# Attention scores: 64x64 TensorE tiles for each head's first 64 channels, 32-row tiles for the last 16

## The chip, the core and the metric

The kernel runs on one core of one Trainium2 chip. Five engines work side by side and meet at semaphores: TensorE (PE, matrix products, with its weight loads listed apart as PEld), VectorE (DVE), ScalarE (ACT), GpSimd (POOL) and SyncE (SP, which issues most DMAs). The metric is the device time of one execution in microseconds. TensorE multiplies a stationary operand, the weights, with a moving operand that streams through; the result goes to PSUM, whose banks are named s_ps, q_ps and so on here. A product may use only a part of the array's rows and columns, a tile, and products on different tiles may run side by side.

## What is computed

For each of 16 batch elements: 100 queries of width 640 attend over 718 keys of width 384 with 8 heads of 80 channels, a second attention over 4 extra tokens is added, and an output projection, a bias and the input follow.

```python
query = hidden_states @ Wq
keyt = enc @ Wk
valt = enc @ Wv
hs = _mha(query, keyt, valt)          # 8 heads, softmax over 718 keys
...
ca_hs2 = _mha(ca_q2, ca_k2, ca_v2)    # the 4 tokens
out = hs + ca_hs2
out = out @ Wout + b_out
out = out + residual
```

The change concerns `scores = einsum('bhqd,bhkd->bhqk', qh, kh)` inside the first `_mha`: for each head, 80 channels of the query times 80 channels of each key.

## The kernel before

All data are float32, and a float32 product appears in the trace as two TensorE records. The order of all instructions on all engines is written out by hand in the source: what stands earlier is issued earlier on its engine.

**Layout of the 640 channels.** Queries and keys are held with channels on the 128 partitions, in five chunks of 128. The columns of Wq and the rows of the transposed Wk (`wkt`) are permuted so that a chunk holds what the score products need. In chunks 0 to 3 a band of 32 partitions holds 32 of a head's first 64 channels: `packed` (line 104) puts heads 2r and 2r+1 into band r, the even one into chunks 0 and 1, the odd one into chunks 2 and 3. Chunk 4 holds the last 16 channels of all eight heads, so that a band of 32 partitions has two heads.

**Start.** `load_heads` (line 299) issues eight DMAs of 64 rows of `wkt`, alternating between the queues of ScalarE and SP; one more DMA on SP (line 307) brings chunk 4. `turn_back` (line 586) transposes each chunk of `wkt` on TensorE into w_ps, `first_keys` multiplies the first element's context with them. The permuted copies of Wq into `wq_sb` (lines 1277 to 1289) are made on ScalarE, two copies of 256 columns and one of 128 for each of five row chunks. DMAs take eight semaphores in turn, and a DMA waits for the one that had its semaphore before.

**One batch element.** `queries` (line 540) makes the projected queries of two elements: `qp` for chunks 0 to 3 and `qz` for chunk 4. `qz` holds two versions of the queries side by side, each with the other head's channels set to zero, so one product with 200 columns serves both heads of a band. Keys lie in six chunks of 120 (`KC`). `scores` (line 646) runs three times for each element, g = 0, 1, 2, and each time covers two key chunks, a = 0, 1. For each a it goes through the five channel chunks and the four bands: in chunks 0 to 3 a product with 32 rows, 120 key columns as weights and 100 streamed query columns, in chunk 4 one with 200 streamed columns. Band r always writes PSUM bank r, in which heads 2r and 2r+1 lie side by side; a call has 40 products. Groups 0 and 2 use two pairs of banks from the same pool, which ScalarE copies to `st` in two copies (line 688); group 1 uses four other banks and four copies (line 682).

After the scores come z_ps and y_ps of the second attention, then the blocks of keys (`k_ps`, line 470) and values (`v_ps`, line 439) in a fixed interleaving, then r_ps (line 1546) and a_ps (line 1564), which multiply the exponentials `st` with the values: r_ps in tiles of 32 weight columns, four at a time, for the last 16 channels and the sums, a_ps in tiles of 64 weight columns, two at a time. VectorE takes the maximum over the score tiles (lines 1416 and 1407) and subtracts it (line 1395); ScalarE makes the exponentials (line 1403).

Of the kernel before, what the change touches and what calls it, by code (L numbers as in the profile page):

```python
# [14 lines left out]
B, S, H = 16, 100, 640  # L15
NH, D = 8, 80
CAD, T = 384, 4
SK = 722 - T
P = 128
HC = H // P  # L20
# [3 lines left out]
KN = KT // 2  # L24
# [3 lines left out]
KEYS = [KN if j == 0 or u == 2 else KN - 1 for u, j in KC]  # L28
# [31 lines left out]
for h in range(NH):  # L60
    lo = h * D
    while lo < (h + 1) * D:
        c = lo // P
        hi = min((h + 1) * D, (c + 1) * P)
        PIECES.append((h, c, lo - h * D, lo - c * P, hi - lo))
        lo = hi
# [18 lines left out]
RG = 4  # L85
# [15 lines left out]
            )  # L101


def packed(to, w, h):

    rows = w.rearrange("(h k) n -> h k n", h=NH)
    at, c = 32 * (h // 2), 2 * (h % 2)
    return {
        "out": to[at : at + 32, c : c + 2],
        "in_": rows[h, :64].rearrange("(v k) n -> k v n", v=2),  # L110
    }


V_PLAN = [
# [33 lines left out]
def kernel(  # L148
# [18 lines left out]
    nc = tc.nc  # L167
# [22 lines left out]
    def pair(name):  # L190
        tile = ps2.tile([P, 2, 512], F32, tag="ps2", name=name)
        return tile
# [21 lines left out]
    def scores_tile(name):  # L214
        return main.tile([P, 2, ROWS], F32, tag="st", name=name, bufs=NP)
# [55 lines left out]
    def a_form(enc, f):  # L271
        return enc[0][:, A_AT[f]]
# [4 lines left out]
    wq_sb = const.tile([P, HC, H], F32, name="wq_sb")  # L277
    kT = const.tile([P, HC, 3, KT], F32, name="kT")
# [11 lines left out]
    wkt_sb = kT.rearrange("p c u k -> p c (u k)")[:, :, :CAD]  # L290
# [6 lines left out]
        )  # L297

    def load_heads(u):
        for h in range(u, NH, 2):  # L300
            (nc.scalar, nc.sync)[h // 2 % 2].dma_start(**packed(wkt_sb, wkt, h))

    load_heads(0)
    load_first(nc.sync, 0, 0)
    load_first(nc.scalar, 1, 0)
    load_first(nc.sync, 2, 0)
    load_heads(1)
    nc.sync.dma_start(
        out=wkt_sb[:, 4], in_=wkt.rearrange("(h k) n -> h k n", h=NH)[:, 64:]
    )  # L310
    for c in range(1, CC):
        for u in range(3):
            load_first(nc.sync, u, c)
# [9 lines left out]
        out=wv_sb[:, : 2 * CC].rearrange("p (c g) n -> p c (g n)", g=2),  # L323
        in_=wv.rearrange("(c p) n -> p c n", p=P),
# [6 lines left out]
    wq_in = [t[:, :H] for t in halves]  # L331
# [9 lines left out]
    def slot(i, h, lo, n):  # L341

        u, j = KC[i]
        lo += h % 4 * SLOT
        return vs.rearrange("p j k h n -> p j k (h n)")[: KEYS[i], j, 2 * u + h // 4, lo : lo + n]
# [16 lines left out]
    for h, c, r, s, k in PIECES:  # L362
        nc.gpsimd.dma_start(
            out=m2[s : s + k, c, GROUPS[c][1].index(-1), h * T : (h + 1) * T],
            in_=wqcat[h * D + r : h * D + r + k, :],
# [4 lines left out]
    for c in range(HC):  # L370
        first = c * P - HEADS[c][0] * D
        nc.gpsimd.affine_select(
            out=hmask[:, c], in_=hmask[:, c], compare_op=ALU.is_ge, fill=0.0,
# [3 lines left out]
            out=hmask[:, c], in_=hmask[:, c], compare_op=ALU.is_ge, fill=0.0,  # L377
# [37 lines left out]
    class Values(Blocks):  # L415
# [17 lines left out]
        def product(self, at, f, first, last):  # L433
            for bank in "AB":
                if self.opened[bank] is at and bank in self.fresh:
                    first = True
                    self.fresh.discard(bank)
            for j in range(2):
                nc.tensor.matmul(  # L439
                    at[0][j][:KN, : H // 2],  # L440
                    a_form(self.enc, f)[:, j * KN : (j + 1) * KN],
                    wv_sb[:, W_AT[f]],
                    start=first,
                    stop=last,
                    skip_group_check=True,
                )
# [199 lines left out]
    def scores(b, g, tiles):  # L646

        qp, qz = tiles
        name = f"s_ps_{b}_{g}"
        if g == 1:  # L650
            s_ps = [f(f"{name}_{r}") for r, f in enumerate((psumk, psumk, psum1, psum1))]
        else:
            pairs = [pair(f"{name}_{i}") for i in range(2)]
            s_ps = [pairs[r // 2][:, r % 2] for r in range(RG)]
        n = KN
        opened = set()

        def product(a, c, rows, bank, lo, rhs, last):
            u, j = KC[2 * g + a]
            nc.tensor.matmul(  # L660
                s_ps[bank][:n, 256 * a + lo : 256 * a + lo + rhs.shape[-1]],
                kT[rows, c, u, j * KN : (j + 1) * KN],
                rhs,
                start=bank not in opened,
                stop=last,
                skip_group_check=True,
            )
            opened.add(bank)

        for a in range(2):  # L670
            for c in range(HC):
                for r in range(RG):
                    rows = slice(32 * r, 32 * r + 32)
                    if c < HC - 1:
                        rhs = qp[rows, c // 2, c % 2, (b % 2) * S : (b % 2 + 1) * S]
                        product(a, c, rows, r, c // 2 * S, rhs, False)
                    else:
                        product(a, c, rows, r, 0, qz[rows, 0, b % 2], True)
        st = scores_tile(f"st_{b}_{g}")[:n]
        if g == 1:  # L680
            for r in range(RG):
                nc.scalar.copy(  # L682
                    st[:, :, 2 * r * S : 2 * (r + 1) * S],
                    s_ps[r][:n].rearrange("p (a q) -> p a q", a=2)[:, :, : 2 * S],
                )
        else:
            for i in range(2):
                nc.scalar.copy(  # L688
                    st[:, :, 4 * i * S : 4 * (i + 1) * S].rearrange(
                        "p a (r q) -> p r a q", r=2  # L690
                    ),
                    pairs[i][:n].rearrange("p r (a q) -> p r a q", a=2)[:, :, :, : 2 * S],
                )
        return st
# [580 lines left out]
        del gaps[:n]  # L1275

    for c in range(HC):
        for u in range(2):
            nc.scalar.copy(
                wq_sb[:, c, 2 * u * P : 2 * (u + 1) * P].rearrange(  # L1280
                    "p (v r k) -> p r v k", v=2, r=RG
                ),
                wq_in[c].rearrange("p (r u k) -> p r u k", r=RG, u=2)[
                    :, :, u, :64
                ].rearrange("p r (v k) -> p r v k", v=2),
            )
        nc.scalar.copy(
            wq_sb[:, c, 4 * P :].rearrange("p (h k) -> p h k", h=NH),
            wq_in[c].rearrange("p (h k) -> p h k", h=NH)[:, :, 64:],
        )  # L1290

    k2_ps = psum("k2_ps")
    for n in range(HC):
        for c in range(CC):
            for lo in (0, 64):
# [4 lines left out]
                    start=(c == 0),  # L1300
                    stop=(c == CC - 1),
                )
    k2T, at = [], 0
# [14 lines left out]
    for c in range(HC):  # L1318
        m_ps = psum(f"m_ps_{c}")
        for n, heads in enumerate(HEADS):  # L1320
# [4 lines left out]
                start=(n == 0),  # L1325
# [31 lines left out]
    for c in range(HC):  # L1357
        for half in range(2):
            h = 2 * c + half
            for cc in range(CC):  # L1360
                if c < HC - 1:
                    lo = h * D + FIRST[half]
                    weights = wvca_sb[:, cc, lo : lo + 64]
                else:
# [5 lines left out]
                    start=(cc == 0),  # L1370
# [5 lines left out]
    last, late, second_next = None, False, Second(1, xT)  # L1376
    for b in range(B):
        p = b // 2
# [13 lines left out]
        st = []  # L1392
# [12 lines left out]
        def larger(i):  # L1405
# [4 lines left out]
            return most_now  # L1410

        st.append(scores(b, 0, tiles))
        waiting = late
        if late:
            now.exponentials1()
        nc.vector.tensor_tensor(most[:KN], st[0][:, 0], st[0][:, 1], ALU.max)  # L1416
        st.append(scores(b, 1, tiles))
        larger(1)
        if b == 0:
            now.exponentials1()  # L1420
        st.append(scores(b, 2, tiles))

        vv = Values(b, e_in, V_PLAN if b + 1 < B else END_PLAN)
# [118 lines left out]
        for i in order:  # L1542
            for e in range(2):
                for h in range(e, NH, 2):
                    at = 16 * (h - e)
                    nc.tensor.matmul(  # L1546
                        rests[at : at + 32, e],
                        slot(i, h, -16 if e else 64, 32),
                        st[i // 2][: KEYS[i], i % 2, h * S : (h + 1) * S],
                        start=(i == order[0] and e == 0),  # L1550
                        stop=(i == order[-1]),
                        skip_group_check=True,
                    )
# [7 lines left out]
        for i in range(len(KC)):  # L1561
            for h in range(NH):
                e = h % 2
                nc.tensor.matmul(  # L1564
                    wides[64 * e : 64 * e + 64, h // 2],
                    slot(i, h, FIRST[e], 64),
                    st[i // 2][: KEYS[i], i % 2, h * S : (h + 1) * S],
                    start=(i == 0 and h // 2 == 0),
                    stop=(i == len(KC) - 1),
                    skip_group_check=True,  # L1570
                )
# [9 lines left out]
        last = mine  # L1581
# [52 lines left out]
```

## Time and profile before

| | us |
|---|---|
| three timed runs: median (lowest to highest) | 921.77 (920.55 to 922.27) |
| profiled execution: its own time | 921.04 |
| profiled execution: span of the trace | 919.3 |

A page of the profile gives busy time by engine, then the chain of work that ended last, then groups of instructions. In a group's row stand the line, the engine, the operation, out<-in by name, the rows*columns of the weights, the shape of the moving operand, the count, then busy time in us and the mean of one in ns. Busy time is the time in which at least one such instruction ran; with several tiles at once it is far below count times mean. Rows of the chain and of the timeline begin with the start and the length in us. A matmul's recorded length contains its way through the array; how fast matmuls follow one another is read from starts and counts.

### The profile page before, as it was taken

Reading aid. Unit: us, or ns where it says so; the run is one execution under the profiler, and the core shown is the slowest. Engines: PE = TensorE matmul, PEld = TensorE weight load, DVE = VectorE, ACT = ScalarE, POOL = GpSimd, SP = SyncE. Lnnn points to the kernel's source line nnn. Section 1 sums busy time; section 2 is a strip of 40 time slices with the busy share of each in tenths; the row PEclk is TensorE's granted clock in tenths of the full one; section 3 lists DMA queues with packets and bytes.
Section 4 is the critical chain, followed back from the end, with each engine's and each line's share of the span. In section 5 each row is a group of like instructions: output and inputs, shape, how many; then the busy total and the mean of one; then the engine's idle time right before and its main releaser. Section 6 shows DMA issues by size and latency. Waiting matters only on the chain.

```text
span 919.3 us, 26076 instructions
## 1 busy us (share of the span) xinstructions
PE 912.0 (99%) x11155; PEld 776.6 (84%) x11155; DVE 665.5 (72%) x1121; ACT 376.6 (41%) x654; POOL 620.6 (68%) x653
## 2 busy tenths in 40 slices
PE   8999999999999999999999999999999999999998
PEld 8988889797887979888798788988888888888865
DVE  3898795979639696675957759579782887828773
ACT  2354533544324443433434334344541445425351
POOL 9665786677847788476774756755796566955735
PEclk9999999999999999999999999999999999999999
DMA  9604351141402313140221403205140151401312
GB/s 288 218 11 133 66 123 34 29 120 39 103 12 70 106 25 90 43 132 12 72 72 43 132 12 81 71 6 134 43 110 11 34 140 36 111 11 45 86 53 64
DMA packets 68060, 69.50 MB, mean 76 GB/s; under 512 B 25192, under 2 KB 61352, under 8 KB 67944
## 3 DMA queue, kind: packets, MB, share of 16 engines
q1 hardware_dynamic: 67016, 66.97, 27.2%
q8 instruction: 88, 1.44, 0.7%
q10 hardware_dynamic: 464, 0.52, 0.2%
q0 software_dynamic: 464, 0.34, 0.2%
q14 instruction: 28, 0.23, 0.1%
HBM read 62.14 MB, written 8.94 MB: 77 GB/s over the span
## 4 chain that ended last, share of the span: by engine, by line
PE 97%; DMA 1%; POOL 1%; ACT 0%; DVE 0%; issue 0%; ACTq 0%; SPq 0%; DVEq 0%; POOLq 0%
PE s_ps L660 12%; PE v_psA L439 11%; PE v_psB L439 9%; PE k_psA L470 8%; PE a_ps L1564 7%; PE q_ps L544 7%; PE k_psB L470 7%; PE kT_ps L568 6%; PE r_ps L1546 4%; PE v_psC L439 4%; PE k_psC L470 3%; PE y_ps L799 2%; PE v_psD L439 2%; PE o_psy L1128 2%; PE v_psE L439 2%; PE k_psE L470 1%
## 5 line engine op out<-in xcount | busy, mean ns | idle before, releaser
L834 POOL TENSOR_TENSOR e<-ca,g 100x800 f32<-100x800 f32 x60 | 91.8, 1540 | 101.0 <-DVE most L1407 74.3
L439 PE MATMUL v_psA<-wv_sb,enc 128*120 128x320 f32 x384 | 119.6, 434 | 0.0
L507 POOL TENSOR_TENSOR enc<-enc 128x240 f32<-128x240 f32 x144 | 108.7, 765 | 8.0
L439 PE MATMUL v_psB<-wv_sb,enc 128*120 128x320 f32 x320 | 99.2, 432 | 0.0
L660 PE MATMUL s_ps<-qp,kT 32*120 32x100 f32 x3072 | 97.4, 263 | 0.0
L660 PEld LDWEIGHTS s_ps<-qp,kT 32*120 32x120 f32 x3072 | 94.7, 179 | 1.9
L841 POOL TENSOR_TENSOR e<-e,e 100x800 f32<-100x800 f32 x45 | 92.2, 2048 | 3.5
L439 PEld LDWEIGHTS v_psA<-wv_sb,enc 128*120 128x120 f32 x384 | 69.0, 183 | 24.7 <-DVE vs L410 0.9
L1395 DVE TENSOR_TENSOR st<-st,over 120x1600 f32<-120x1600 f32 x46 | 88.8, 1930 | 0.0
L470 PE MATMUL k_psA<-enc,wk_sb 128*128 128x240 f32 x360 | 87.6, 366 | 0.0
L470 PEld LDWEIGHTS k_psA<-enc,wk_sb 128*128 128x128 f32 x360 | 68.4, 190 | 17.1
L1407 DVE TENSOR_TENSOR most<-most,st 120x800 f32<-120x800 f32 x64 | 63.3, 990 | 21.7 <-ACT st L682 20.4
L439 PEld LDWEIGHTS v_psB<-wv_sb,enc 128*120 128x120 f32 x320 | 58.6, 183 | 23.4
L1403 ACT ACTIVATE st<-st 120x1600 f32<-120x1600 f32 x48 | 73.9, 1540 | 8.2 <-DVE st L1395 5.7
L470 PE MATMUL k_psB<-enc,wk_sb 128*128 128x240 f32 x300 | 73.0, 366 | 0.0
L1416 DVE TENSOR_TENSOR most<-st 120x800 f32<-120x800 f32 x16 | 17.3, 1082 | 76.6 <-ACT st L688 76.6
L1564 PE MATMUL a_ps<-st,vs 120*64 120x100 f32 (+1 forms) x1536 | 69.5, 250 | 0.0
L544 PE MATMUL q_ps<-xT,wq_sb 128*128 128x200 f32 x400 | 69.1, 332 | 0.0
L1564 PEld LDWEIGHTS a_ps<-st,vs 120*64 120x64 f32 (+1 forms) x1536 | 66.4, 137 | 2.7 <-issue 2.7
L544 PEld LDWEIGHTS q_ps<-xT,wq_sb 128*128 128x128 f32 x400 | 68.0, 190 | 0.2
L412 ACT COPY vs<-v_psA 120x640 f32<-120x640 f32 x48 | 33.3, 693 | 83.8 <-PE v_psA L439 83.7
L688 ACT COPY st<-s_ps 120x800 f32<-120x800 f32 x64 | 49.7, 829 | 43.4 <-PE s_ps L660 43.4
(183 smaller groups left out, 1886.2 us busy)
## 6 DMA issues: line engine op xcount, KB each, us to landing
pb<-p_d SPq DMA_DIRECT2D x32, 400.0 KB
enc<-in_enct SPq DMA_DIRECT2D x30, 240.0 KB
enc<-in_enct SPq DMA_DIRECT2D x15, 360.0 KB
xT<-in_xt SPq DMA_DIRECT2D x8, 500.0 KB
rest<-in_enct SPq DMA_DIRECT2D x31, 120.0 KB
xn<-in_x SPq DMA_DIRECT2D x11, 320.0 KB
wide_d<-p_d SPq DMA_DIRECT2D x16, 200.0 KB
pb<-wide_d SPq DMA_DIRECT2D x16, 200.0 KB
```

The lines of the kernel that those rows point to most:

```text
L439: nc.tensor.matmul(at[0][j][:KN, : H // 2], a_form(self.enc, f)[:, j * KN : (j + 1) * KN], wv_sb[:, W_AT[f]], start=first, stop=last, skip ...
L470: nc.tensor.matmul(at[:, i * KT : (i + 1) * KT], wk_sb[:, W_AT[f], i], a_form(self.enc, f), start=(first and i == 0), stop=last, skip_grou ...
L507: first = nc.gpsimd.tensor_tensor(out, left, right, op)
L544: nc.tensor.matmul(q_ps[:, : 2 * S].rearrange("p (j s) -> p j s", j=2), wq_sb[:, c, n * P : (n + 1) * P], xT[:, :, c, :], start=(c == 0), ...
L568: nc.tensor.matmul(bank[:, i * KT : (i + 1) * KT], weights[c], a_raw(enc, u, c), start=(i == 0 and c == 0), stop=(c == CC - 1), skip_group ...
L660: nc.tensor.matmul(s_ps[bank][:n, 256 * a + lo : 256 * a + lo + rhs.shape[-1]], kT[rows, c, u, j * KN : (j + 1) * KN], rhs, start=bank not ...
L834: first = engine.tensor_tensor(to, self.ca[:, t, :].unsqueeze(1).to_broadcast([S, NH, S]), g[:, :, t].unsqueeze(2).to_broadcast([S, NH, S] ...
L841: engine.tensor_tensor(e, e, to, ALU.add)
L1395: return engine.tensor_tensor(st[i], st[i], top.over[:KN].unsqueeze(1).to_broadcast([KN, 2, ROWS]), ALU.subtract,)
L1403: nc.scalar.activation(st[i], st[i], AF.Exp, scale=SCALE)
L1407: most_now = nc.vector.tensor_tensor(most[:KN], most[:KN], st[i][:, u], ALU.max)
L1564: nc.tensor.matmul(wides[64 * e : 64 * e + 64, h // 2], slot(i, h, FIRST[e], 64), st[i // 2][: KEYS[i], i % 2, h * S : (h + 1) * S], start ...
```

## The change

Heads are laid out by parity: even heads on partitions 0 to 63, odd heads on 64 to 127, chunk c holding heads 2c and 2c+1, each with its first 64 channels on 64 adjacent partitions. Chunk 4 is ordered likewise, even heads first. `load_heads` loads heads 0 to 3 before the first context pieces and heads 4 to 7 after them, even heads on ScalarE's queue and odd ones on SP's, and chunk 4 comes in two DMAs of 64 partitions. The copies of Wq for chunks 0 to 3 become one copy of 512 columns for each row chunk.

In `scores` a product of the first 64 channels takes 64 rows and one half of the key chunk, 64 or 56 columns: 4 chunks x 2 parities x 2 halves = 16 products for each a, as many as before. Even heads go to banks 0 and 1, odd ones to banks 2 and 3. The products of chunk 4 keep their 32 rows and 120 columns. They no longer follow each a; a call does all heads' products and then all of chunk 4 (`others`) in groups 0 and 2, and the reverse in group 1. `PLACE` gives the place of a head in `st`, which r_ps and a_ps now use.

```diff
+PLACE = [4 * (h % 2) + h // 2 for h in range(NH)]
 def packed(to, w, h):
     rows = w.rearrange("(h k) n -> h k n", h=NH)
-    at, c = 32 * (h // 2), 2 * (h % 2)
-    return {
-        "out": to[at : at + 32, c : c + 2],
-        "in_": rows[h, :64].rearrange("(v k) n -> k v n", v=2),
-    }
+    return {"out": to[64 * (h % 2) : 64 * (h % 2) + 64, h // 2], "in_": rows[h, :64]}
...
     def load_heads(u):
-        for h in range(u, NH, 2):
-            (nc.scalar, nc.sync)[h // 2 % 2].dma_start(**packed(wkt_sb, wkt, h))
+        for h in range(4 * u, 4 * u + 4):
+            (nc.scalar, nc.sync)[h % 2].dma_start(**packed(wkt_sb, wkt, h))
...
-    nc.sync.dma_start(
-        out=wkt_sb[:, 4], in_=wkt.rearrange("(h k) n -> h k n", h=NH)[:, 64:]
-    )
+    for e in range(2):
+        nc.sync.dma_start(
+            out=wkt_sb[64 * e : 64 * e + 64, 4],
+            in_=wkt.rearrange("(c e k) n -> e c k n", e=2, k=D)[e, :, 64:],
+        )
...
-        def product(a, c, rows, bank, lo, rhs, last):
+        def product(a, c, rows, keys, bank, lo, rhs, last):
             u, j = KC[2 * g + a]
+            first = [k for k in (0, 64) if keys.start <= k < keys.stop and (bank, k) not in opened]
             nc.tensor.matmul(
-                s_ps[bank][:n, 256 * a + lo : 256 * a + lo + rhs.shape[-1]],
-                kT[rows, c, u, j * KN : (j + 1) * KN],
+                s_ps[bank][keys, 256 * a + lo : 256 * a + lo + rhs.shape[-1]],
+                kT[rows, c, u, j * KN + keys.start : j * KN + keys.stop],
                 rhs,
-                start=bank not in opened,
+                start=bool(first),
                 stop=last,
                 skip_group_check=True,
             )
-            opened.add(bank)
-
-        for a in range(2):
-            for c in range(HC):
+            opened.update((bank, k) for k in first)
+
+        def heads(last):
+            for a in range(2):
+                for c in range(HC - 1):
+                    for e in range(2):
+                        at = 4 * e + c
+                        rows = slice(64 * e, 64 * e + 64)
+                        rhs = qp[rows, c // 2, c % 2, (b % 2) * S : (b % 2 + 1) * S]
+                        for keys in (slice(0, 64), slice(64, n)):
+                            product(a, c, rows, keys, at // 2, at % 2 * S, rhs, last)
+
+        def others(last):
+            for a in range(2):
                 for r in range(RG):
                     rows = slice(32 * r, 32 * r + 32)
-                    if c < HC - 1:
-                        rhs = qp[rows, c // 2, c % 2, (b % 2) * S : (b % 2 + 1) * S]
-                        product(a, c, rows, r, c // 2 * S, rhs, False)
-                    else:
-                        product(a, c, rows, r, 0, qz[rows, 0, b % 2], True)
+                    product(a, HC - 1, rows, slice(0, n), r, 0, qz[rows, 0, b % 2], last)
+
+        for k, part in enumerate((others, heads) if g == 1 else (heads, others)):
+            part(k == 1)
...
     for c in range(HC):
-        for u in range(2):
-            nc.scalar.copy(
-                wq_sb[:, c, 2 * u * P : 2 * (u + 1) * P].rearrange(
-                    "p (v r k) -> p r v k", v=2, r=RG
-                ),
-                wq_in[c].rearrange("p (r u k) -> p r u k", r=RG, u=2)[
-                    :, :, u, :64
-                ].rearrange("p r (v k) -> p r v k", v=2),
-            )
         nc.scalar.copy(
-            wq_sb[:, c, 4 * P :].rearrange("p (h k) -> p h k", h=NH),
-            wq_in[c].rearrange("p (h k) -> p h k", h=NH)[:, :, 64:],
+            wq_sb[:, c, : 4 * P].rearrange("p (h k) -> p h k", h=NH),
+            wq_in[c].rearrange("p (h k) -> p h k", h=NH)[:, :, :64],
+        )
+        nc.scalar.copy(
+            wq_sb[:, c, 4 * P :].rearrange("p (e h k) -> p e h k", e=2, k=16),
+            wq_in[c].rearrange("p (h e k) -> p e h k", e=2, k=D)[:, :, :, 64:],
         )
...
-                        st[i // 2][: KEYS[i], i % 2, h * S : (h + 1) * S],
+                        st[i // 2][: KEYS[i], i % 2, PLACE[h] * S : (PLACE[h] + 1) * S],
```

The last pair of lines stands in both r_ps and a_ps.

More of the change, by code (lines that the diff above doesn't have):

```diff
@@ L1566 @@
                     slot(i, h, FIRST[e], 64),
-                    st[i // 2][: KEYS[i], i % 2, h * S : (h + 1) * S],
+                    st[i // 2][: KEYS[i], i % 2, PLACE[h] * S : (PLACE[h] + 1) * S],
                     start=(i == 0 and h // 2 == 0),
```

## The prediction

> **What bounds the kernel now.** I read the page's busy times first, then its chain of waits, then the chain in order of time for one batch element.
>
> ```profile
> span 919.3 us, 26076 instructions
> PE 912.0 (99%) x11155; PEld 776.6 (84%) x11155; DVE 665.5 (72%) x1121; ACT 376.6 (41%) x654; POOL 620.6 (68%) x653
> PE 97%; DMA 1%; POOL 1%; ACT 0%; DVE 0%; issue 0%; ACTq 0%; SPq 0%; DVEq 0%; POOLq 0%
> ```
>
> The chain in order of time, one element and one q_ps block (start, length, what):
>
> ```profile
> 85.26 3.65 PE kT_ps L568 x18
> 88.90 2.21 PE r_ps L1546 x96
> 91.12 4.28 PE a_ps L1564 x96
> 95.39 7.28 PE s_ps L660 x240
> 102.67 0.68 PE z_ps L861 x56
> 136.45 8.46 PE q_ps L544 x50
> ```
>
> TensorE carries 97% of the chain, and in the rows of one element nothing stands between its blocks. A nanosecond taken from a TensorE block should therefore come off the end, as long as nobody else becomes late. The scores block (s_ps, 7.28 us) recurs 16 times. A float32 product is two records here: 120 products make the 240 records. The question is which part of 7.28 us is not the streaming of columns.
>
> The pace of streaming: q_ps needs 8.46 / 50 = 169 ns for a record of 200 columns, and kT_ps 3.65 / 18 = 203 ns for 240, both 0.846 ns a column. A record of 100 columns thus needs 84.6 ns, one of 200 needs 169 ns. Within the scores block the timeline of TensorE shows:
>
> ```profile
> 97.42 0.54 PE L660 MATMUL s_ps<-qz,kT 32*120 32x200 f32 x8
> 97.78 1.00 PE L660 MATMUL s_ps<-qp,kT 32*120 32x100 f32 x32
> 98.60 0.54 PE L660 MATMUL s_ps<-qz,kT 32*120 32x200 f32 x8
> ```
>
> The first column is the start. From 97.42 to 97.78, 0.36 us, eight 200-column records run; from 97.78 to 98.60, 0.82 us, thirty-two 100-column records. They run four at a time, one in each band of 32 rows. I call four such records a pass. Two qz passes take 0.36 us, near 2 x 169 ns. Eight qp passes take 0.82 us, where streaming would take 8 x 84.6 = 0.68 us. The missing 0.14 us over the seven passes that follow another 100-column pass is 20 ns each, so their pace is 105 ns. What lasts 105 ns? The groups of weight loads by shape say:
>
> ```profile
> L660 PEld LDWEIGHTS s_ps<-qp,kT 32*120 32x120 f32 x3072 | 94.7, 179 | 1.9
> L1564 PEld LDWEIGHTS a_ps<-st,vs 120*64 120x64 f32 x1024 | 45.3, 137 | 2.7 <-issue 2.7
> L1546 PEld LDWEIGHTS r_ps<-st,vs 120*32 120x32 f32 x1024 | 22.6, 110 | 5.7 <-issue 5.0 <-ACT st L1403 0.8
> L544 PEld LDWEIGHTS q_ps<-xT,wq_sb 128*128 128x128 f32 x400 | 68.0, 190 | 0.2
> ```
>
> The means grow from 110 ns at 32 weight columns to 190 ns at 128, (190 - 110) / 96 = 0.83 ns a column. Loading 120 key columns thus occupies a band for 100 ns, longer than the 84.6 ns for which the loaded weights are used. The scores block is bound by its weight loads, and 64 columns would take 53 ns and hide.
>
> **The change, part by part, against the profiled execution's 921.04 us (span 919.3; the three timed runs have a median of 921.77).**
>
> *Passes of the first 64 channels.* Their number stays: 2 key chunks x 4 channel chunks x 4 tiles x 2 records = 64 records, 16 passes, for each of three score groups of an element, 48 passes in all. A tile of 64 rows by 64 or 56 columns replaces one of 32 rows by 120. No 64x64 tile runs in the trace of before, so its pace has to be bounded. The lower bound is the stream, 84.6 ns. The nearest row for the upper bound is the present pace, 105 ns. The nearest rows altogether are those with 64-column loads and those with four tiles at once: a_ps runs 48 pairs in 4.28 us, at most 89 ns a pair, with two 64-column loads on the same rows for each pair; r_ps runs 24 fours in 2.21 us, at most 92 ns, with its switch of shape in it. The s_ps rows show that bands of rows load side by side, the a_ps rows that column halves do. I take 84.6 ns. Stalls removed: an element's block now consists of six halves of 0.82 + 0.36 us, 7.08 us, against 48 x 84.6 + 12 x 169 ns = 6.09 us of streaming. That is 0.99 us an element.
>
> *Switches of tile shape.* A group now has two shapes, and the order heads-others, others-heads, heads-others puts three switches inside each block that were not there. What does entering a new shape cost? Above streaming, r_ps pays 2.21 - 24 x 84.6 ns = 0.18 us, a_ps 4.28 - 48 x 84.6 ns = 0.22 us, s_ps 7.28 - 7.08 = 0.20 us. Three of three pay it, which excludes a free switch; the lower bound is 0.18 us. The upper bound is a load and a product wholly in series, less the stream, from these means:
>
> ```profile
> L660 PE MATMUL s_ps<-qp,kT 32*120 32x100 f32 x3072 | 97.4, 263 | 0.0
> ```
>
> 179 + 263 - 85 = 0.36 us. I take 0.20 us, what the entry to these same tiles costs: 3 x 0.20 = 0.60 us an element. The entry from a_ps and the exit to z_ps stay. The Trainium skill (TensorEngine Tiling (Array Packing), Key Properties) says that changing the tiling mode, not merely the tile, drains TensorE. It prices nothing. The three entries above agree with it, and without that rule the sum would lose its 0.60 us term.
>
> *Sum of the block:* 6.09 + 0.20 + 0.60 = 6.89 us against 7.28, a gain of 0.39 us; 16 elements give 6.2 us.
>
> *Start.* The weights wkt come in pieces of the same size, but the last 16 channels of all heads now arrive in two DMAs instead of one, issued one behind the other on SP's queue (first SP's issues in the timeline, then the start of the chain):
>
> ```profile
> 4.97 0.78 SPq L308 DMA_DIRECT2D kT<-in_wkt  x1
> 6.07 2.25 SPq L294 DMA_DIRECT2D enc<-in_enct  x5
> 4.97 5.03 DMA kT<-in_wkt
> 10.13 0.52 PE w_ps L589 x3
> ```
>
> That DMA's landing at 10.00 releases TensorE at 10.13. Half a DMA takes half of 0.78 us to issue, but the program hands its DMAs eight semaphores in turn, and each waits for its semaphore's last DMA. The second half takes the place of the enc load which now starts at 6.07, 0.32 us after SP was free. If it also starts at 6.07 and lands 4.25 us after its issue, as the whole one does, it is there at 10.7, 0.7 us late. If its half size makes up for that, nothing is lost. I take 0.3 us. The enc loads queued behind it on SP move by up to 0.4 us, as does TensorE. That chunks 0 and 1 need only two pieces each saves nothing, since TensorE waits at 10.13 in any case.
>
> *Edits at nothing.* Ten copies of wq become five on ScalarE:
>
> ```profile
> 25.38 0.71 ACT L1279 COPY wq_sb<-wq 128x256 f32<-128x256 f32 x2 [2.11 <-DMA wq<-in_wq]
> 29.72 0.29 ACT L1287 COPY wq_sb<-wq 128x128 f32<-128x128 f32 x1
> 25.50 6.91 PE m_ps L1321 x50
> 32.41 1.69 PE q_ps L544 x10
> ```
>
> The last ends at 30.01, under m_ps; q_ps, which reads wq_sb, starts at 32.41, so 2.4 us of cover hide them. Uncovered, the five copies would be worth at most 5 x 0.4 us. The other order of heads in st only changes which 100 columns r_ps and a_ps stream: same counts, same shapes.
>
> *Who becomes late next?* The third group reuses the banks of the first, which ScalarE copies out:
>
> ```profile
> 98.04 1.55 ACT L688 COPY st<-s_ps 120x800 f32<-120x800 f32 x2 [2.11 <-PE s_ps L660]
> 99.97 0.37 PEld L660 LDWEIGHTS s_ps<-qp,kT 32*120 32x120 f32 x8
> ```
>
> The copies end at 99.59, the load starts at 99.97: 0.38 us of slack. The second group between them shrinks from 2.36 us to 16 x 84.6 + 4 x 169 ns + 0.20 = 2.23 us, and 0.25 us is left. ScalarE at 41% and VectorE at 72% have room for 0.39 us less in each element.
>
> 921.04 - 6.2 + 0.3 = 915.1 us as profiled, and 915.9 from the median. I say **915.6**.
>
> **The rivals.**
>
> *A. Two loads in one band queue up (slower).* The two key halves of a 64-row band share their rows. If their loads ran in turn, a pass would last 2 x 53 = 107 ns. That adds 22 ns x 48 x 16 = 17 us: 932.6. It decides from 0.39 us / 48 = 8 ns on, at a pace above 93 ns. Against it stands a_ps, whose two 64-column loads on common rows fit in 89 ns. For it: no row shows row bands and column halves together. Chance 0.07.
>
> *B. A load waits for the stream in its band.* A pass is then 53 + 85 = 138 ns, and 53 ns x 768 = 41 us more: 956.5. The q_ps rows speak against it: loads of 128 columns in the very rows that stream, yet 169 ns a record, all of it stream. Chance 0.02. This is the rule of the Trainium skill (TensorE: Matmul & The Clock Gate, The mechanism) that weight loads overlap running products only in another row group; the trace does not agree with it here.
>
> *C. A switch costs 0.33 us or more,* near its upper bound: gain and price cancel. At 0.36 us it adds 0.16 x 48 = 7.7 us: 923.3; so 920 to 923. The entries at 0.18 to 0.22 us speak against it. Chance 0.06.
>
> *D. The change does not do what it says:* the 105 ns come from something other than the columns loaded, and the pace stays. 20.4 ns x 768 = 15.7 us more: 931.3. The 0.36 us for two qz passes, loaded alike, show that the bound vanishes once the stream is longer. Chance 0.04.
>
> *E. The gain is partly swallowed* by ScalarE: if a copy ended 0.2 us after TensorE wants its bank, 3.2 us go: 918.8. Chance 0.03.
>
> **How the numbers follow.** Forecast 0.78. Its own range: switches at 0.18 to 0.25 us give -1.0 to +2.4 us, the start -0.3 to +0.4: 913.5 to 918. A measurement of this kernel can tell 0.2%, 1.8 us, from no change. Faster: 0.78 + 0.03 = 0.81; no change: C, 0.06; slower: A, B and D, 0.13. The range of 913.0 to 920.5 takes in E and the lower end of C and leaves out A, B, D and the rest of C, under 0.2. The far bounds of pace and switch lie in those rivals.
>
> **What would show it.** The trace of after should show sixteen 64x64 passes in about 1.36 us; loads of 64 columns at about 137 ns; s_ps blocks of about 6.9 us in the chain; gaps of about 0.2 us above stream where 32-row and 64-row tiles meet; w_ps of the last chunk at 10.1 to 10.8. A pace of 105 to 107 ns would prove the forecast wrong, as would gaps of 0.3 us, or a ScalarE copy releasing a score tile.

## The result, and the profile after

| | before | after |
|---|---|---|
| median of 6 runs each on one chip (lowest to highest), us | 921.20 (920.55 to 922.64) | 917.56 (916.16 to 918.75) |
| profiled execution: its own time / span, us | 921.04 / 919.3 | 917.43 / 915.7 |

The ratio of after to before is 0.9961, with a 95% interval of 0.9951 to 0.9971: 3.6 us faster. That lies inside the range given and 2.0 us above the number forecast. So something gave back over a third of the 6.2 us expected from the scores blocks.

The page of after, busy times and chain:

```profile
span 915.7 us, 26079 instructions
PE 906.2 (99%) x11155; PEld 762.9 (83%) x11155; DVE 667.3 (73%) x1121; ACT 375.4 (41%) x649; POOL 621.1 (68%) x653
PE 97%; DMA 1%; POOL 1%; DVE 0%; issue 0%; ACT 0%; SPq 0%; ACTq 0%; DVEq 0%; POOLq 0%
```

TensorE still carries 97% of the chain. The chain in order of time, the same element as shown for before:

```profile
86.37 3.65 PE kT_ps L570 x18
92.22 4.28 PE a_ps L1571 x96
96.49 6.87 PE s_ps L663 x147
103.36 0.64 PE z_ps L873 x52
```

The scores block is 6.87 us, where it was 7.28; its neighbours keep their lengths. Inside that block, the timeline of TensorE (start, length, group, count):

```profile
96.42 1.60 PE L663 MATMUL s_ps<-qp,kT 64*64 64x100 f32 x64
97.95 1.63 PE L663 MATMUL s_ps<-qz,kT 32*120 32x200 f32 x32
99.51 2.97 PE L663 MATMUL s_ps<-qp,kT 64*64 64x100 f32 x128
102.41 0.95 PE L663 MATMUL s_ps<-qz,kT 32*120 32x200 f32 x16
103.30 0.75 PE L873 MATMUL z_ps<-y,e 100*32 100x33 f32 x64
```

The order heads, others-others, heads-heads, others can be read off: 64, 32, 128 and 16 records. From one start to the next, 64 records (16 passes) take 1.53 us and 128 records (32 passes) take 2.90 us, each with one switch in it. The difference, 1.37 us for 16 passes, is 85.6 ns a pass, so the stream sets the pace. With streaming at 84.6 and 169 ns taken off, the three switches are 1.53 - 1.35 = 0.18, 1.56 - 1.35 = 0.21 and 2.90 - 2.71 = 0.19 us.

The weight loads by shape:

```profile
L663 PEld LDWEIGHTS s_ps<-qp,kT 64*64 64x64 f32 x1536 | 67.0, 133 | 5.9 <-issue 3.9
L663 PEld LDWEIGHTS s_ps<-qp,kT 64*56 64x56 f32 x1536 | 66.6, 127 | 0.0
```

The means are 133 and 127 ns, where it was 179 ns for 120 columns. So far all is as forecast. Two other places are not. The waits of TensorE (what waits, on what, us in total, times, longest):

```profile
PE w_ps L591 <- DMA kT<-in_wkt: 2.2, 2, 2.0
PE z_ps L873 <- issue: 1.5, 3, 0.7
PE y_ps L811 <- issue: 0.2, 1, 0.2
```

In before, w_ps waited 0.8 us in all, and z_ps 0.2 us for "issue", which means that nothing the profile shows held it. The first row belongs to the start. Chain and timeline there (SP's issue of the two halves, the landing, the transposes, the rest of the first keys):

```profile
5.47 1.28 SPq L309 DMA_DIRECT2D kT<-in_wkt  x2
6.19 5.26 DMA kT<-in_wkt
11.58 0.52 PE L591 MATMUL w_ps<-e,kT 128*128 128x128 f32 x3 [1.97 <-DMA kT<-in_wkt]
12.10 11.79 PE kT_ps L622 x58
```

The second half of chunk 4 is issued at 6.19 and lands 5.26 us later, at 11.45. kT_ps begins at 12.10 where it began at 10.65, so the start is 1.45 us late. The chain of before, shown with the prediction, has the whole of chunk 4 issued at 4.97 and landed 5.03 us later. So the 1.45 us are 0.50 for a first half that is issued later (5.47 for 4.97), 0.72 from the issue of the first half to that of the second, and 0.23 for a longer way from issue to landing. The second and third rows of the waits lie behind the scores blocks; in element 3:

```profile
206.19 0.71 PE L873 MATMUL z_ps<-y,e 100*32 100x33 f32 x58
207.63 0.26 PE L873 MATMUL z_ps<-y,e 100*32 100x33 f32 x6 [0.72 <-issue]
```

The same place in before:

```profile
206.38 0.71 PE L861 MATMUL z_ps<-y,e 100*32 100x33 f32 x58
207.31 0.26 PE L861 MATMUL z_ps<-y,e 100*32 100x33 f32 x6 [0.21 <-issue]
```

After 58 of 64 products TensorE stands still, in both kernels at the same product, but 0.5 us longer in after. I laid the two traces side by side, tile by tile. Such standstills (start-to-start gaps inside z_ps or y_ps) add up to 1.21 us in before (elements 2, 3, 8, 10, 11) and to 2.48 us in after (elements 3, 8, 10, 11). The bill of the spans: blocks -6.46 us, start +1.45, standstills +1.27, together -3.7; measured 915.7 - 919.3 = -3.6.

They fall in the trace at instructions whose number in TensorE's stream (weight loads, matmuls and the instructions that handle semaphores) is 193 modulo 256. That is the spacing of the packets of the queue called "instruction":

```profile
q8 instruction: 88, 1.44, 0.7%
```

1.44 MB in 88 packets is 16.4 KB each. One such packet starts between 205 and 206 us, just ahead of the standstill. Hence the theory S that I tested: TensorE runs out of instructions there, because the shorter scores block followed by z_ps consumes 256 of them faster than a block of them comes. Eight such boundaries fall into z_ps or y_ps in after, and four of them have a standstill.

### The profile page after: what moved, and what is told of

It is laid out like the page before. It is cut to its first block, busy times and chain, and to the rows that moved or that the text cites. A ratio compares the mean times of both kernels' runs of the same rounds, so it can differ in the third digit from the quotient of the medians.

```text
span 915.7 us, 26079 instructions
## 1 busy us (share of the span) xinstructions
PE 906.2 (99%) x11155; PEld 762.9 (83%) x11155; DVE 667.3 (73%) x1121; ACT 375.4 (41%) x649; POOL 621.1 (68%) x653
## 3 DMA queue, kind: packets, MB, share of 16 engines
q8 instruction: 88, 1.44, 0.7%
## 4 chain that ended last, share of the span: by engine, by line
PE 97%; DMA 1%; POOL 1%; DVE 0%; issue 0%; ACT 0%; SPq 0%; ACTq 0%; DVEq 0%; POOLq 0%
PE s_ps L663 12%; PE v_psA L441 11%; PE v_psB L441 9%; PE k_psA L472 8%; PE a_ps L1571 7%; PE q_ps L546 7%; PE k_psB L472 7%; PE kT_ps L570 6%; PE r_ps L1553 4%; PE v_psC L441 4%; PE k_psC L472 3%; PE y_ps L811 2%; PE v_psD L441 2%; PE o_psy L1140 2%; PE v_psE L441 2%; PE k_psE L472 1%
## 5 line engine op out<-in xcount | busy, mean ns | idle before, releaser
L663 PE MATMUL s_ps<-qp,kT 64*56 64x100 f32 (+1 forms) x3072 | 73.3, 248 | 0.0
L663 PEld LDWEIGHTS s_ps<-qp,kT 64*56 64x56 f32 (+1 forms) x3072 | 67.0, 130 | 5.9 <-issue 3.9
```

Source lines behind the costliest of these rows:

```text
L663: nc.tensor.matmul(s_ps[bank][keys, 256 * a + lo : 256 * a + lo + rhs.shape[-1]], kT[rows, c, u, j * KN + keys.start : j * KN + keys.stop] ...
```

## The experiments

**The changed kernel again.**

> The changed kernel once more, for the stalls of TensorE that stand at fixed places of its instruction stream (207.6, 488.4, 602.0 and 649.2 us in the first trace, 0.2 to 0.9 us each). Theory S, TensorE waits there for the next 16 KB block of its instructions, whose fetch began 2.5 to 2.8 us earlier: the stalls stand at the same instructions again, with lengths that follow the fetch; the ratio to before is 0.996 again. Rival, they are waits for other engines or chance: they stand elsewhere or are gone.

917.55 us against 920.49 for before on that chip, ratio 0.9967 (0.9952 to 0.9982). The gain repeats. The standstills stood at the same numbers of the stream, with other lengths: 0.39, 0.70, 0.39 and 0.81 us in elements 3, 8, 10 and 11, and 0.55 us in element 2, where after had none.

This profiled execution (919.30 us) also shows what a late start can cost beyond the delay itself. TensorE waits 2.2 us for the second half of chunk 4, and then the granted clock (third column from the end) falls:

```profile
11.98 13.45 PE kT_ps L622 x58
12.00:14.00 2.00, 2.00 (x7) 1.72 (x7) 0.39 (x2) 0.48 (x1) 1.81 (x7) 0.56 0.83 227
```

The same kT_ps block takes 11.79 us in after, 1.66 us less, with a clock of 1.00 in that stretch after a wait of 1.97 us.

**Is the weight load the bound, and is it hidden at 64 columns?** Products of 64 rows and all 120 columns, two tiles at once in place of four:

```diff
-                        for keys in (slice(0, 64), slice(64, n)):
+                        for keys in (slice(0, n),):
```

> The first 64 channels in tiles of 64 rows by all 120 key columns, two at a time, half as many products; nothing else changed. Theory L, a pass lasts as long as the longer of loading its weight columns and streaming: 120 columns load in 100 ns, so the pace of passes goes from 86 back to 105 ns, the scores block from 6.87 to about 7.7 us (48 passes x 19 ns = 0.91 more), and the time to about 932 us. Rival, the old 105 ns came from four bands of rows side by side or from the rate of instructions: two bands and half the instructions keep 86 ns or less, and the time stays near 917.5 us or falls.

929.33 us, ratio 1.0095 (1.0075 to 1.0115). The timeline and the chain of its scores block, then its weight loads by shape:

```profile
96.67 1.93 PE L663 MATMUL s_ps<-qp,kT 64*120 64x100 f32 x32
98.52 1.63 PE L663 MATMUL s_ps<-qz,kT 32*120 32x200 f32 x32
100.08 3.60 PE L663 MATMUL s_ps<-qp,kT 64*120 64x100 f32 x64
103.62 0.95 PE L663 MATMUL s_ps<-qz,kT 32*120 32x200 f32 x16
96.74 7.83 PE s_ps L663 x144
```

```profile
L663 PEld LDWEIGHTS s_ps<-qp,kT 64*120 64x120 f32 x1536 | 83.1, 182 | 5.9 <-issue 3.9
```

The same number of passes (16 and 32, now of two records) takes 1.85 and 3.54 us: 1.69 / 16 = 105.6 ns a pass, with the same moving operand and the same 64 rows as in after; the weight columns changed, and with them the tiles at once, two for four. In before it was 105 ns with 120 columns too, there in 32 rows and four tiles at once. So the pace follows the columns loaded, neither the height of the tile nor the number of tiles at once. This is the sum's first term, shown directly. The block is 0.96 us longer than after's, 15.4 us for 16; the total grew by less, 11.8 us against 917.55 on that chip, mainly because it has no standstills in z_ps or y_ps (2.48 us in after) and its start is 0.4 us earlier. It also has 3072 weight loads and matmuls fewer, so its boundaries lie elsewhere; the next run tells more about the standstills.

**What does a switch cost?** The order goes back to one half of a group at a time, so nine switches in a block instead of three:

```diff
-        def heads(last):
-            for a in range(2):
+        def heads(last, half):
+            for a in half:
...
-        for k, part in enumerate((others, heads) if g == 1 else (heads, others)):
-            part(k == 1)
+        for half in ((0,), (1,)):
+            for k, part in enumerate((others, heads) if g == 1 else (heads, others)):
+                part(k == 1, half)
```

> Heads and others in turn for each of the two key chunks of a group, so nine switches of tile shape inside an element's scores block instead of three. If a switch costs what the trace of after shows (0.20 us into the 32-row tiles, 0.16 us into the 64-row tiles), three more of each add 1.08 us an element, 17 us in all: about 935 us, and the gain is gone. With the 0.36 us of the prediction's upper bound: 952 us. If a switch is nearly free and the lost gain lies elsewhere: within 3 us of 917.5.

932.32 us, ratio 1.0128 (1.0107 to 1.0148). Its block in the chain:

```profile
96.75 7.96 PE s_ps L663 x155
```

7.96 - 6.87 = 1.09 us for six more switches, 0.18 us each. Over the 16 blocks that is 17.0 us, and the time grew by 14.8 us against 917.55 on that chip, almost 3 us less than expected. The standstills make up most of the rest: this kernel has as many instructions as after and its boundaries fall at the same products, yet there is no standstill at any of the eight in z_ps and y_ps. Slower scores blocks at the same boundaries leave no standstill, as theory S has it. The run also bounds what merging the groups is worth: without the order heads, others-others, heads-heads, others the change would have lost time, not won it.

**Fewer, larger loads at the start.** Each chunk of 128 partitions of the key weights in one transfer (two heads), the halves of chunk 4 as in after:

```diff
-        for h in range(4 * u, 4 * u + 4):
-            (nc.scalar, nc.sync)[h % 2].dma_start(**packed(wkt_sb, wkt, h))
+        rows = wkt.rearrange("(c e k) n -> c e k n", e=2, k=D)
+        for c in range(2 * u, 2 * u + 2):
+            (nc.scalar, nc.sync)[c % 2].dma_start(out=wkt_sb[:, c], in_=rows[c, :, :64])
```

> The start: one DMA of 128 partitions for each of chunks 0 to 3 instead of two of 64; chunk 4 stays in two. Theory Q, the start is set by how long SP is busy issuing (0.47 to 0.82 us for each DMA of 64 partitions, 0.78 us for the one of 128 in the kernel before): SP needs about 2.2 us less ahead of the last piece of chunk 4, which lands about 2 us earlier than 11.45 us, and the time falls by 1.5 to 2 us to about 915.8. Rival B, the bytes moved set it: the same bytes, so the landing stays at 11.4 and the time at 917.5.

932.22 us, ratio 1.0127 (1.011 to 1.0144): a miss for every theory I had then. TensorE's first keys (timeline), and the second half of chunk 4 in the chain:

```profile
10.02 0.88 PE L592 MATMUL w_ps<-e,kT 128*128 128x128 f32 x3 [5.52 <-DMA kT<-in_wkt]
20.81 0.52 PE L592 MATMUL w_ps<-e,kT 128*128 128x128 f32 x3 [1.86 <-DMA kT<-in_wkt]
11.03 11.62 DMA kT<-in_wkt
```

The chip moved little meanwhile. The queue with the loads issued on SP, between 8 and 10 us in this kernel (packets, MB, share of 16 engines):

```profile
q1 hardware_dynamic: 34, 0.05, 6.9%
```

and in after between 4 and 5 us, where the loads of single heads run on the same queue:

```profile
q1 hardware_dynamic: 183, 0.16, 54.3%
```

6.9% of 16 engines is 1.1 engines, 54.3% is 8.7; the queue of ScalarE has 5.9% and 48.9%. What sets this apart is the outermost dimension of the source: 2 slices here (two heads), 64 for a single head's rows. That gave theory K: a transfer spreads over no more engines than its outermost slices allow. The Trainium skill (DMA: Bandwidth & Descriptors, Why a DMA increments its semaphore by 16 and not by 1) states such a rule: as many engines, up to 16, as divide the outermost sizes of both sides. With 2 slices it gives 2 engines, and the trace with 1.1 of them busy agrees. By it, each half of chunk 4 in after (4 slices of 16 rows) gets 4 engines where before's single transfer (8 slices) gets 8. Whether that costs time is the question of the next run.

**Undo only the load of chunk 4.** One transfer with heads outermost, as in before; the order by parity is made on the way out of w_ps:

```diff
-    for e in range(2):
-        nc.sync.dma_start(
-            out=wkt_sb[64 * e : 64 * e + 64, 4],
-            in_=wkt.rearrange("(c e k) n -> e c k n", e=2, k=D)[e, :, 64:],
-        )
+    nc.sync.dma_start(
+        out=wkt_sb[:, 4], in_=wkt.rearrange("(h k) n -> h k n", h=NH)[:, 64:]
+    )
...
+        for e in range(2):
+            (nc.scalar.copy, nc.vector.tensor_copy)[e](
+                wk4[:, :, 64 * e : 64 * e + 64].rearrange("p a (c k) -> p a c k", k=16),
+                w_ps[:, : CC * P].rearrange("p (a c e k) -> p a c e k", a=CC, e=2, k=16)[
+                    :, :, :, e
+                ],
+            )
```

> Of the change only the load of the fifth chunk of the key weights is undone: it comes as one transfer again, heads outermost (8 slices, in place of two transfers of 4 slices each), and the order by even and odd heads is made in the copy of w_ps_4 into wk4, in two halves. Theory K (a transfer keeps only as many packets under way as its outermost slices allow, so the two halves crawl): w_ps_4 waits no longer for kT by 2 us, the first kT_ps of the chain begins at 10.6 to 10.9 us (11.79 in the changed kernel, 10.65 -> 11.79 in its chain's terms against 12.10 now), and the time is 1.2 to 1.4 us below the changed kernel's: about 916.2. Theory I (the two issues on SP, 0.6 us each, delay what stands behind them): the weights come only some 0.5 us earlier, time about 917. Stalls of TensorE in z_ps stay as they are in both (0.4 to 0.9 us in four or five elements).

> The kernel with the fifth chunk's load in one transfer once more, for the comparison on one chip: 917.1, first kT_ps of the chain at 10.9 to 11.1 us, and stalls in z_ps at elements 3, 8 and 11 of 0.4 to 0.8 us.

917.10 us, ratio 0.9958 (0.9944 to 0.9971), and on another chip 916.06, ratio 0.9950 (0.9938 to 0.9962). The chain of the second profile:

```profile
5.31 4.56 DMA kT<-in_wkt
10.00 0.52 PE w_ps L589 x3
10.52 12.02 PE kT_ps L629 x58
```

kT_ps begins at 10.52; in the first profile it begins at 11.07, after a load that was issued at 5.86 and took 4.55 us to land. Against 12.10 that is 1.0 to 1.6 us. 0.23 us of it goes back inside kT_ps (12.02 for 11.79): two of its products start 0.35 and 0.31 us after the one before, in place of about 0.2, and the first of them waits for VectorE's half of the copies into wk4. The spans are 914.8 and 913.9, where after's is 915.7. Of the standstills expected in the second profile that in element 8 did not come, and elements 2 and 10 had one (0.54 and 0.32 us).

Is it the slices (theory K) or the issues on SP (theory I)? The traces whose start is otherwise nearly alike can be put side by side (us; the last is the run with three idle products below):

| chunk 4 in | run | first issue | last issue | from last issue to landing | landed at |
|---|---|---|---|---|---|
| two halves | after | 5.47 | 6.19 | 5.26 | 11.45 |
| two halves | the changed kernel again | 5.31 | 6.02 | 5.30 | 11.32 |
| two halves | 120 columns | 5.70 | 6.42 | 4.67 | 11.08 |
| two halves | nine switches | 4.78 | 5.50 | 5.46 | 10.96 |
| one transfer | before | 4.97 | 4.97 | 5.03 | 10.00 |
| one transfer | this run, first | 5.86 | 5.86 | 4.55 | 10.41 |
| one transfer | this run, second | 5.31 | 5.31 | 4.56 | 9.87 |
| one transfer | three idle products | 4.94 | 4.94 | 5.43 | 10.38 |

The halves always land later, at 10.96 to 11.45 against 9.87 to 10.41. Between the two issues of halves lie 0.71 to 0.72 us. From the last issue to the landing the ranges overlap, 4.67 to 5.46 us for halves and 4.55 to 5.43 us for whole transfers. So the extra issue is shown. A part for the number of slices is not shown here: half the bytes take about as long as all of them, which fits theory K, but also a time set by something else. The times do not decide either: 917.10 is near theory I's 917, 916.06 near theory K's 916.2. And the three ratios of kernels with one transfer or two (0.9958 and 0.9950 against 0.9961) have intervals that overlap, so the whole times do not show the gain at the start; the traces do.

**Move the boundaries of the instruction blocks.** 56 small idle products at the start in place of seven of 128 columns, 196 instructions more ahead of everything:

```diff
-    for _ in range(7):
-        nc.tensor.matmul(idle_ps[:, :P], idle, idle, start=True, stop=True)
+    for k in range(56):
+        at = 32 * (k % 4)
+        nc.tensor.matmul(
+            idle_ps[at : at + 32, :32], idle[:, :32], idle[:, :32], start=True, stop=True
+        )
```

> The changed kernel with its seven idle products of 128 columns at the start replaced by 56 of 32 columns, so that TensorE's stream has 196 more instructions and each boundary of 256 instructions falls elsewhere in the elements. Theory S (TensorE runs out of instructions at such a boundary where it consumes them fastest, right behind the score blocks): the stalls in z_ps and y_ps at elements 2, 3, 8, 10 and 11 are gone or have moved to other elements at other places of the stream (elements 0 and 6 are likely), and the sum of them falls by 0.5 to 1.3 us: time 916.3 to 917.1. Theory T (the stalls belong to the data, such as a late y copy): they stand at the same elements and products, time as now, 917.5.

917.26 us, ratio 0.9956 (0.994 to 0.9971). The median says little; the trace says more. The same z_ps of element 3:

```profile
209.18 0.75 PE L873 MATMUL z_ps<-y,e 100*32 100x33 f32 x64
```

All 64 products run in one piece. Against after, laid side by side, elements 3, 8, 10 and 11 gain 0.95, 0.45, 0.39 and 0.76 us, and element 0 loses 0.58, which was one of the two named ahead. Work and data are the same, only the position in the stream moved; theory T falls and S holds. (That the wait is for the packet itself follows from the order of events: the packet's start lies 2.5 to 2.8 us ahead of the end of each standstill in after.) In the chain the kT_ps block that begins at 36.51 in after and the end of the span show the sum:

```profile
39.09 3.67 PE kT_ps L570 x18
```

2.58 us late at 39 us, 916.2 - 915.7 = 0.5 us late at the end: 2.1 us won in between. The 2.6 us were lost by the edit itself, at the start:

```profile
3.63 0.87 PE L591 MATMUL w_ps<-e,kT 128*128 128x128 f32 x3 [0.42 <-DMA kT<-in_wkt]
8.22 1.14 PE L622 MATMUL kT_ps<-enc,wk_sb 128*128 128x240 f32 x2 [2.57 <-DMA enc<-in_enct]
9.15 1.01 PE L622 MATMUL kT_ps<-rest,wk_sb 128*128 128x240 f32 x2
```

The context pieces land late. An instruction packet now moves at 4 to 5 us, where after has none, and occupies one DMA engine for 1.7 us; that this is what delays them is argued, not shown. And two records of kT_ps take 0.8 to 0.9 us instead of 0.41.

**Both edits together.**

> The two edits together: the fifth chunk's load in one transfer with the even and odd order made in the copies into wk4, and 56 small idle products in place of seven. If theories K and S both hold the gains add: 1.2 to 1.4 us from the start and 0.5 to 1.3 us from the boundaries, 914.9 to 915.8; if only K holds, about 916.2; if neither, 917.5.

917.07 us, ratio 0.9960 (0.9948 to 0.9973): the gains did not add, since the late context pieces came again (2.06 us of waiting). The slow kT_ps has its cause here, as is seen in windows of 2 us (length, TensorE busy, loads, VectorE, ScalarE, GpSimd, granted clock, DMA share, GB/s):

```profile
6.00:8.00 2.00, 0.01 (x1) 0.00 (x0) 0.56 (x1) 0.00 (x0) 1.61 (x4) 0.97 0.59 123
8.00:10.00 2.00, 1.92 (x5) 1.70 (x6) 0.00 (x0) 0.00 (x0) 1.25 (x3) 0.50 0.72 207
```

After a stretch in which TensorE did next to nothing, its clock is granted at 0.50. In the run with the 56 idle products alone, the same windows show 1.00 beside the slow kT_ps, so that the clock is the cause there too is not shown.

**Boundaries moved without that price.** On top of the single load of chunk 4, three idle products of 300 columns instead of seven of 128: as much work at the start, 16 instructions fewer.

```diff
-    for _ in range(7):
-        nc.tensor.matmul(idle_ps[:, :P], idle, idle, start=True, stop=True)
+    for _ in range(3):
+        nc.tensor.matmul(idle_ps[:, :300], idle[:, :P], idle, start=True, stop=True)
```

> The kernel with the fifth chunk's load in one transfer, and its seven idle products of 128 columns replaced by three of 300: TensorE is kept busy at the start for as long (900 columns for 896), with 16 instructions fewer ahead of the elements, so each boundary of 256 instructions falls 16 instructions later. Theory S, with the stalls seen so far between the 46th and the 141st instruction from the first z_ps of an element: the boundaries at 137 and 139 (elements 2 and 10) move out of that stretch, those at 92, 117, 119 (elements 8, 3, 11) stay in it: stalls fall by some 0.3 to 0.9 us, time 916.2 to 916.8 where the seven products gave 917.1. The start stays as it is, first kT_ps of the chain at 10.9 to 11.1 us. Theory T (stalls belong to elements): no change, 917.1.

915.93 us, ratio 0.9942 (0.993 to 0.9954), beside 916.06 for the seven products in the same comparison: no difference that can be told, and not the 0.3 to 0.9 us expected. The places moved as theory S has it. The boundaries of elements 2 and 10 now fall into v_psA, with no standstill seen there; that of element 3 moved from z_ps into y_ps and took its standstill along:

```profile
205.19 0.75 PE L880 MATMUL z_ps<-y,e 100*32 100x33 f32 x64
205.86 1.56 PE L818 MATMUL y_ps<-m,xT 128*100 128x96 f32 x10
```

y_ps is 1.56 us long, where it is 1.21 in after. About 1.35 us of standstills stay (elements 3, 8, 11), some 0.5 us less than in the second profile of the single load alone; but here kT_ps begins at 11.03, 0.5 us later than there. This kernel and the one with the single load alone had the lowest times, on a chip on which the changed kernel itself was not run; their ratios do not stand clear of its ratio.

Not tried: the old tiles in the new layout of heads, which would undo the tiles alone. The new layout and the new tiles were thus told apart only through the terms, not by a run of their own. The run with 120 columns comes nearest: in the new layout the block took 7.83 us, and the gain was gone.

## Why the prediction came out as it did

- *The bound.* Right. Weight loads of 120 columns held the pace at 105 ns; with 64 and 56 columns it is 85.6, forecast 84.6. The run with 120 columns in 64-row tiles brought 105.6 back.
- *The switches.* Right: 0.18, 0.21 and 0.19 us against 0.20 each, and 0.18 for each of six more.
- *The block.* 6.87 us in the chain against the forecast of 6.89.
- *Who becomes late next.* The answer "nobody on ScalarE" holds: group 2 of the scores starts without a gap, and no score tile waits for a ScalarE copy in the waits of TensorE. What became late instead was the supply of instructions, which the prediction did not have. The shorter block made the standstills behind it longer, from 1.21 to 2.48 us: 1.3 us of the missing gain. The row of it stood in the trace of before, 0.21 us of "issue" in front of six z_ps products, and I had passed over it as too small.
- *The start.* This term was mis-sized: +0.3 us was taken, up to 0.7 its far end, +1.45 the measurement. "Half a DMA takes half of 0.78 us to issue" was wrong: the first half took 0.67 us. That its issue would begin at 4.97 as before was wrong too: it began at 5.47, because the piece whose landing SP waited for landed at 4.94 instead of 4.58, and the issue right ahead took 0.47 us instead of 0.33. (In the table above it begins anywhere from 4.78 to 5.86 in the new layout, so this part changes from one execution to the next.) The second issue began at 6.14, near the 6.07 that was said, but that was luck: the prediction had SP free and waiting for a semaphore, and in the trace SP was busy with the first half until then. And the half size did not make up for anything: 5.26 us from issue to landing, where the whole took 5.03, and 4.70 us from the end of the issue, where 4.25 was reckoned. So w_ps of the last chunk began at 11.58, outside the 10.1 to 10.8 that was named. The run with one transfer gave 1.0 to 1.6 us back.
- *The rivals.* A (93 ns and more a pass) and B (138 ns) fell with 85.6 ns; D fell with the same number and with the 120-column run; C needed 0.33 us a switch; E needed a late ScalarE copy. E's number of 918.8 came nearest to the measurement, for another reason than its own.
- *The sums.* They come out when redone, but for one: from 915.1, -1.0 and -0.3 give 913.8 as the low end of its own range, not 913.5. Nothing rests on it.

So the direction and the mechanism were right. The sum for the profiled execution was 915.1 us, its time is 917.43. Two terms make up 2.2 of the difference of 2.3: 1.45 - 0.3 = 1.15 us at the start and 1.27 us of standstills, less 0.26 us that the blocks gained beyond the 6.2. That the time stayed inside the range with a larger start and the standstills was in part luck: the room on that side was meant for dearer switches and a late ScalarE copy, and neither came.

## What to carry to other kernels

When a product moves fewer columns than its weights have, look at the weight load as the bound, and narrow the tile until it hides; then count the switches of tile shape and group the products so that few are left, at some 0.2 us each. When a load is cut in two, count the extra issue on the path of the last piece, 0.7 us here, and do not count on half the bytes landing sooner. Do not leave a load with only two slices in its outermost dimension. And when a stretch of small products gets faster, look for rows of "issue" behind it before counting on all of the gain.

## What the hardware showed that was not expected

- *Instruction supply can hold TensorE up.* At some of the 256th instructions of its stream, where fast small products come together, it stands still for 0.2 to 0.9 us, at fixed places for one program and with varying lengths. The Trainium skill (Runtime: NRT & Kernel Launch, Instruction fetch mechanics) has the 16 KiB blocks of 256 instructions and calls their cost mostly hidden; the block size agrees with the 16.4 KB packets, and the hiding with most of the 88 packets, but not with the four boundaries named for after.
- *Transfers of few slices crawl.* 2 outermost slices: 1.1 of 16 engines busy, and 11.62 us from issue to landing for a half chunk of 96 KB behind such loads. With 4 slices or 8 no difference is shown: 4.67 to 5.46 us and 4.55 to 5.43 us.
- *TensorE's clock can fall to half after a short rest.* A rest of 2.06 us, after sparse work, was followed by a granted clock of 0.50 in the next two microseconds, and in the changed kernel run again one of 2.2 us by a clock of 0.56. A rest of 1.97 us in after was not: 1.00.
